# Layer 0's power chains with a scale at every third squaring, and its products entered by two channel chunks at a time

## The chip, the cores and the metric

The kernel runs on one core of a Trainium2 chip. The metric is the device time of one execution in microseconds (us). A core has a matrix engine (TensorE, in the profile PE, its weight loads PEld), a vector engine (VectorE, DVE), an engine for activation functions (ScalarE, ACT), a general engine (GpSimd, POOL) and a queue engine for transfers (SyncE, SP). Each engine takes its instructions in order; they wait for each other by semaphores.

## What is computed

The reference passes x, 8 images of 512 channels by 1024 pixels in float32, through four layers. Only Layer 0 is touched by the change:

```python
z = jnp.einsum('bcn,bcm->bnm', f_x, g_x)          # f_x, g_x: 64 x 1024 for each image
S = jnp.linalg.svd(z, compute_uv=False)
sigma = S[:, 0][:, None, None]                    # the largest singular value
z2 = jnp.einsum('bnm,bcm->bcn', z / sigma, h_x).reshape(b, MID, h, w)
return conv1x1(z2, Wv, bv) + x
```

Layer 1 is a group normalisation and an attention over 1024 pixels, Layer 2 an attention with 128 channels, Layer 3 a convolution of signs.

## The kernel before

**Layer 0's chain.** The largest singular value of z = f'g comes from powers of the 64 x 64 matrix (ff')(gg'), whose largest eigenvalue is sigma squared. Two images stand side by side as blocks of one 128 x 128 matrix (a pair, j), so there are four chains. `chain(j, split)` is a generator. It keeps the current power and its transpose, `cur[:, 0]` and `cur[:, 1]`. A squaring is `products` (two 128x128 matmuls, L1008 and L1009) and `evict` (PSUM to SBUF). In the kernel before, NSTEP is 11: after a first product come 22 squarings, a `yield` after each. Every second one is followed by `diagonal` (VectorE: product with the identity, L1036, and a sum over the row, L1037), and its sum over the partitions, `total`, is a matmul with a 128x1 operand (L1042) and a copy into `tr` (L1043). Its reciprocal (L1069) and the products of it (L1070) scale the next scaled eviction (L1030, or L1026 on ScalarE). At the end the logarithms of the traces (L1080), weighted by `quarters`, give 1/sigma, which scales the weights of the pair's images.

**Who runs the chains.** The chain of the pair whose images come first (`jl`, images 6 and 7) runs in the early stage, in an order of TensorE written out by hand: after each step of the chain some steps of `todo` (weight products L1265, transposes L1117, Gram matrices L1312, biases L1290) are taken as fillers. The other three (`behind = chains()`) run inside the main loop `fast(n)`, one for each image in the order 6, 7, 0, ..., 5: `chore(2)` takes one step of `behind` at every second step of a stage.

**The main loop.** `fast` has the stages scores of Layer 1 (`scores1`, 28 steps of two 128x512 matmuls at L380, here called terms), V (`make_v`, 14 steps at L380), values (`values1`, 14 steps at L547), and then Layers 2 and 3 together with the next image's first products. A term's result is moved out of PSUM by VectorE (`plus`, L337) or by ScalarE. Each bank of PSUM holds 128x512 numbers; the main loop has eight.

**Entering the next image.** `entering(n)` makes Layer 0's last product for image n: `weights0` (L282, evicted at L285 or L287), and then `enter`. For each of four chunks of 128 channels, `enter` does one visit: two matmuls of 64 rows, one for each half of the pixels, on the upper and the lower half of TensorE's rows (L403); then for each half an addition of x (L412) and statistics (L415), and an aggregate (L416). Two further steps make the group normalisation's mean (L423) and its deviation (L430), which give the scale and bias that `normal` applies. In `fast` the six steps are taken at k = 12, 15, 18, 21, 24 and 27 of `scores1`. In the early stage image 6 is entered by `steps`, with fillers between.

Outside the hand-written part and a few marked instructions, a planner sets each engine's order from the program's order and its own estimates. The image's x is loaded on the SP queue after the last image's rest (`rest3`) is done, in four transfers of 512 KB.

Of the kernel before, what the change touches and what calls it, by code (L numbers as in the profile page):

```python
# [8 lines left out]
F32 = mybir.dt.float32  # L9
F16 = mybir.dt.float16  # L10
I32 = mybir.dt.int32
AF = mybir.ActivationFunctionType
# [4 lines left out]
P = 128  # L17
# [47 lines left out]

NSTEP = 11

# [14 lines left out]
def kernel(  # L84
# [36 lines left out]
    def bank():  # L121
        return psum["bank"].tile([P, HF], F32, tag="bank", name="bank")
# [85 lines left out]
    minus_half = const.tile([P, CC], F32, tag="minus_half", name="minus_half")  # L208
    nc.gpsimd.memset(minus_half, -0.5)

    quarters = const.tile([P, NSTEP], F32, tag="quarters", name="quarters")
    for s in range(NSTEP):
        nc.gpsimd.memset(quarters[:, s : s + 1], 0.25**s)

    def vec(name):
        return ct[:, COL[name] : COL[name] + CC]
# [174 lines left out]

    weights = {}

    def enter(xt, f, pv):

        st = stat.tile([P, CC, NH, 6], F32, tag="st1", name="st1")
        mv = stat.tile([P, CC, 2], F32, tag="mv1", name="mv1")
        for oc in range(CC):  # L400
            banks = [bank() for h in range(NH)]
            for h, ps in enumerate(banks):
                mm(  # L403
                    out=ps,
                    lhsT=pv[side(h), bass.ts(oc, P)],
                    rhs=f[side(h), :],
                    start=True,
                    stop=True,
                )
            for h, ps in enumerate(banks):  # L410
                xs = xt[:, oc, half(h)]
                nc.vector.scalar_tensor_tensor(  # L412
                    xs, ps, bvo[:, oc : oc + 1], xs, ALU.add, ALU.add
                )
                nc.vector.bn_stats(st[:, oc, h, :], xs)  # L415
            nc.vector.bn_aggr(mv[:, oc, :], st[:, oc, :, :])  # L416
            yield

        ps = bank()
        mean = stat.tile([P, CC], F32, tag="mean1", name="mean1")  # L420
        dev = stat.tile([P, CC], F32, tag="dev1", name="dev1")
        nc.vector.tensor_tensor(mv[:, :, 0], mv[:, :, 0], bo, ALU.subtract)
        mm(out=ps[:, 0:CC], lhsT=gmat, rhs=mv[:, :, 0], start=True, stop=True)  # L423
# [12 lines left out]
        nc.vector.tensor_tensor(bi, vec("L1_conv_beta"), bi, ALU.subtract)  # L436
        norm[:] = sc, bi
        yield
# [374 lines left out]
    def inverse_sums(env, esum, row):  # L813

        ps = bank()
        for h in range(NH):
            mm(  # L817
                out=ps[side(h), :],
                lhsT=ones2[:, 0:MID],
                rhs=esum[:, half(h)],  # L820
                start=True,
                stop=True,
            )
        r = env["small"].tile([P, HF], F32, tag="rsum", name="rsum", bufs=1)
# [25 lines left out]
    def entering(n):  # L850

        b = order[n]
        f = load_f(b)

        def steps():
            while b // 2 not in ready:
                next(behind)
            if b % 2 == 0:
                for i in (b, b + 1):
                    pvs[i] = weights0(i)  # L860
            yield from enter(resident[b], f, pvs.pop(b))

        return steps()

# [3 lines left out]
    def fast(env, n, hb, ua):  # L868
# [8 lines left out]
        def chore(every):  # L877
            count[0] += 1
            if count[0] % every == 0:
                next(behind, None)  # L880

        es = [None] * NT
        for k, _ in enumerate(scores1(env, hb, ua, es)):
            if rest3 and k % 2 == 0:
                if next(rest3[0], "end") == "end":
                    rest3.pop()
                    if more and order[n + 1] not in resident:
                        resident[order[n + 1]] = load_x(order[n + 1])
            if n == 0 and k == 2:
                weights["o"] = sums_of(quarters_of(wo, chunks, cols2), [so[:, i] for i in range(3)], True)  # L890
            if n == 0 and k == 6:
                tp = quarters_of(sbw["tpg"], chunks, [slice(0, P), slice(P, 2 * P)])
                weights["tp"] = sums_of(tp, [sp[:, i] for i in range(3)], True)
            if k == 8 and more:
                ahead = entering(n + 1)
            if k >= 11 and k % 3 == 0:
                next(ahead, None)
            if not rest3:
                chore(2)
        for _ in ahead:  # L900
# [94 lines left out]
    def chain(j, split):  # L995
# [1 line left out]


        ff, gg, gh = (gm[j][:, i, :] for i in range(3))
        tr = spin.tile([P, NSTEP + 1], F32, tag="tr", name="tr")  # L1000

        def column(name):
            return spin.tile([P, 1], F32, tag=name, name=name)
# [26 lines left out]
                    nc.vector.tensor_scalar(dst, ps, r, again, ALU.mult, ALU.mult)  # L1030
            return cur

        def diagonal(u, v):
            d = spin.tile([P, P], F32, tag="diag", name="diag", bufs=1)
            t = column("tj")
            nc.vector.tensor_tensor(d, u, v, ALU.mult)  # L1036
            nc.vector.tensor_reduce(t, d, AX.X, ALU.add)  # L1037
            return t

        def total(t, s):  # L1040
            ps = bank()
            mm(out=ps[:, 0:1], lhsT=mask2, rhs=t, start=True, stop=True)  # L1042
            nc.vector.tensor_copy(tr[:, s : s + 1], ps[:, 0:1])  # L1043

        t = diagonal(ff, gg)
        got = products(gg, ff)
        total(t, 0)
        r = column("r")
# [10 lines left out]
        t = None  # L1059
# [18 lines left out]
        ln = spin.tile([P, NSTEP], F32, tag="ln", name="ln")  # L1078
        rsig = column("rsig")
        nc.scalar.activation(ln, tr[:, 1:], AF.Ln)  # L1080
        nc.vector.tensor_tensor(ln, ln, quarters, ALU.mult)
        nc.vector.tensor_reduce(rsig, ln, AX.X, ALU.add)
        nc.scalar.activation(rsig, rsig, AF.Exp, scale=-0.125)
        nc.vector.tensor_tensor(rsig, rsig, root, ALU.mult)
        for i in range(2):
            rr = side(i)
# [338 lines left out]
    with tc.manual_schedule(engines={mybir.EngineType.PE}):  # L1425
        steps = entering(0)
        for k, _ in enumerate(chain(jl, True)):
            for _ in range(2 - k % 2 if k <= 2 * NSTEP else 4):
                next(todo, None)
            for args in (next(relus, None),):  # L1430
                if args:
                    relu(*args)
        for k in range(CC + 2):
            next(steps)
            for _ in range(3 if k < CC else 5):
                next(todo, None)
        for _ in todo:
            pass
# [193 lines left out]
```

## Time and profile before

| | |
|---|---|
| median of 14 runs | 1932.19 us (1931.09 to 1933.03) |
| the profiled execution | 1931.56 us |
| its span, first to last instruction | 1929.7 us |
| granted TensorE clock | 0.998 |
| PE busy | 1905.6 us (99%) |
| DVE busy | 1158.4 us (60%) |
| ACT busy | 507.8 us (26%) |
| POOL busy | 229.8 us (12%) |
| DMA | 66.47 MB, 34 GB/s on average |

Busy times are of one profiled execution. A group's line shows the source line, the engine, the operation, output and inputs, the shapes and the count, then busy us and the mean ns of one, then the idle time of the engine just before and what ended it. A float32 matmul stands in the profile as two records, one for each pass. Matmuls are pipelined and their ends are modelled, so durations of neighbours overlap; the distance from start to start is what a piece of work takes. A wait is put down to the semaphore that came last.

### The profile page before, as it was taken

What the parts mean: (1) busy time and instruction counts of PE and PEld (TensorE: products, weight loads), DVE (VectorE), ACT (ScalarE), POOL (GpSimd) and SP (SyncE); (2) the same over time, 40 slices, a digit from 0 to 9 for tenths busy, and PEclk for the clock granted to TensorE, in tenths of its full rate; (3) what the DMA queues carried; (4) which work ended last, traced back from release to release, by engine and by line L of the source; (5) the groups of instructions that cost most, each with busy time, mean ns of one, the idle gap of its engine ahead of it and who ended that gap; (6) DMA issues with size and microseconds to landing.
All of it is one profiled execution on the core that took longest, in us unless ns stands there. A gap on an engine that the chain in (4) does not pass through costs nothing.

```text
span 1929.7 us, 16673 instructions
## 1 busy us (share of the span) xinstructions
PE 1905.6 (99%) x6230; PEld 986.3 (51%) x6230; DVE 1158.4 (60%) x1875; ACT 507.8 (26%) x807; POOL 229.8 (12%) x178
## 2 busy tenths in 40 slices
PE   9999999999999999999999999999999999999997
PEld 3367456544655447454555446544645455544653
DVE  3256677448764687537754676448663775466647
ACT  2141222035222332025212331034202421143114
POOL 0000001200111001300121011201120011201121
PEclk9999999999999999999999999999999999999999
DMA  8420000002000120002000120002000200010001
GB/s 322 152 77 7 1 6 12 1 11 87 17 1 0 33 71 12 1 11 87 17 1 1 33 71 11 1 11 87 11 0 1 86 13 11 0 33 22 11 1 46
DMA packets 27784, 66.47 MB, mean 34 GB/s; under 512 B 4272, under 2 KB 5424, under 8 KB 27056
## 3 DMA queue, kind: packets, MB, share of 16 engines
q1 hardware_dynamic: 26768, 64.90, 10.0%
q8 instruction: 51, 0.84, 0.2%
q10 hardware_dynamic: 864, 0.43, 0.1%
q14 instruction: 37, 0.30, 0.0%
q0 software_dynamic: 64, 0.00, 0.0%
HBM read 38.51 MB, written 18.87 MB: 30 GB/s over the span
## 4 chain that ended last, share of the span: by engine, by line
PE 91%; DVE 7%; ACT 1%; issue 1%; DMA 0%; POOL 0%; DVEq 0%; ACTq 0%
PE bank L380 41%; PE bank L547 20%; PE bank L937 6%; PE bank L796 6%; PE bank L1225 4%; PE bank L648 3%; PE bank L403 2%; PE bank L665 2%; PE bank L1008 1%; PE wide L1265 1%; DVE both L739 1%; DVE both L709 1%; PE bank L1009 1%; PE wide L1312 1%; PE bank L688 1%; PE bank L817 1%
## 5 line engine op out<-in xcount | busy, mean ns | idle before, releaser
L547 PE MATMUL bank<-e,vt 128*128 128x512 f32 x768 | 334.0, 593 | 0.0
L547 PEld LDWEIGHTS bank<-e,vt 128*128 128x128 f32 x768 | 145.0, 190 | 175.4 <-issue 173.2
L380 PE MATMUL bank<-ut,h 128*128 128x512 f32 x384 | 181.3, 596 | 0.0
L337 DVE TENSOR_TENSOR e<-bank,e 128x512 f32<-128x512 f32 x128 | 87.6, 685 | 61.0 <-PE bank L380 60.3
L380 PE MATMUL bank<-us,hs 128*128 128x512 f32 x256 | 122.1, 599 | 1.4 <-DVE us L309 0.5
L380 PEld LDWEIGHTS bank<-ut,h 128*128 128x128 f32 x384 | 71.5, 190 | 85.8 <-issue 83.5
L937 PE MATMUL bank<-e,tpg 128*128 128x512 f32 x256 | 114.7, 595 | 0.0
L796 PE MATMUL bank<-tpg 128*128 128x512 f32 x256 | 114.6, 592 | 0.0
L803 ACT ACTIVATE e<-bank 128x512 f32<-128x512 f32 x128 | 76.4, 597 | 128.5 <-PE bank L796 128.5
L352 POOL TENSOR_TENSOR e<-e 128x512 f32<-128x512 f32 x32 | 44.1, 1379 | 419.5 <-ACT e L331 383.1
L380 PE MATMUL bank<-wo,h 128*128 128x256 f32 x384 | 91.8, 382 | 0.0
L808 DVE TENSOR_TENSOR esum<-esum,e 128x1024 f32<-128x1024 f32 x48 | 58.8, 1226 | 54.5 <-ACT e L803 54.5
L380 PE MATMUL bank<-h,wu 128*128 128x512 f32 x192 | 90.3, 593 | 0.7 <-ACT ut L342 0.7
L337 DVE TENSOR_TENSOR vt<-bank,vt 128x512 f32<-128x512 f32 x64 | 44.1, 688 | 70.4 <-PE bank L380 70.0
L937 PEld LDWEIGHTS bank<-e,tpg 128*128 128x128 f32 x256 | 48.1, 190 | 63.2 <-issue 63.1
L796 PEld LDWEIGHTS bank<-tpg 128*128 128x128 f32 x256 | 48.6, 190 | 60.7 <-issue 60.5
L352 POOL TENSOR_TENSOR ut<-ut 128x512 f32<-128x512 f32 x16 | 21.8, 1360 | 478.2 <-ACT ut L333 478.2
L380 PEld LDWEIGHTS bank<-wo,h 128*128 128x128 f32 x384 | 71.6, 190 | 13.5 <-ACT vt L331 4.1
L380 PEld LDWEIGHTS bank<-us,hs 128*128 128x128 f32 x256 | 46.7, 190 | 56.1 <-issue 46.4
L676 ACT ACTIVATE sg<-xt,rb 128x512 f16<-128x512 f32 x64 | 45.0, 718 | 103.7 <-DVE xt L667 100.2
L825 DVE RECIPROCAL rsum<-bank 128x512 f32<-128x512 f32 x15 | 50.4, 3357 | 28.6 <-PE bank L817 28.6
L380 PE MATMUL bank<-ut,hs 128*128 128x512 f32 x128 | 63.2, 606 | 0.0
(325 smaller groups left out, 3085.2 us busy)
## 6 DMA issues: line engine op xcount, KB each, us to landing
xt<-in_x SPq DMA_DIRECT2D x55, 512.0 KB
out<-both SPq DMA_DIRECT2D x63, 256.0 KB
rfull<-rsum SPq DMA_DIRECT2D x60, 128.0 KB
f_dram<-f SPq DMA_DIRECT2D x8, 256.0 KB
fb<-f_dram SPq DMA_DIRECT2D x8, 256.0 KB
w<-in_w SPq DMA_DIRECT2D x1, 1024.0 KB
q<-in_w_q SPq DMA_DIRECT2D x1, 1024.0 KB
k<-in_w_k SPq DMA_DIRECT2D x1, 1024.0 KB
```

Source lines behind the costliest of these rows:

```text
L337: nc.vector.tensor_tensor(dst, ps, u, ALU.add)
L352: nc.gpsimd.tensor_tensor(c22, c22, c12, ALU.add)
L380: mm(out=ps[:, q * w : (q + 1) * w], lhsT=lt(ka, kb, q, k), rhs=rhs(ka, kb, q, k), start=first and q == 0 and k == 0, stop=last and k == 1 ...
L547: mm(out=ps, lhsT=a[:, t, bass.ts(r_, P)], rhs=e[t], start=first and t == 0, stop=last and t == NTH - 1, skip_group_check=True,)
L648: mm(out=ps[:, i, :], lhsT=xt[:, cc, bass.ts(4 * h + i, P)], rhs=sbw["tpg"][:, cc, 2 * P : 3 * P], start=cc == 0, stop=cc == CC - 1,)
L676: nc.scalar.activation(sg[:, cc, :], xt[:, cc, half(h)], AF.Sign, bias=rb3[:, cc : cc + 1])
L796: mm(out=ps, lhsT=pt[:, 0, bass.ts(t, P)], rhs=tt[:, 0, half(h)], start=True, stop=True,)
L803: nc.scalar.activation(e[:, half(h)], ps, AF.Exp, scale=float(P) ** -0.5)
L808: nc.vector.tensor_tensor(esum, esum, e, ALU.add)
L825: nc.vector.reciprocal(r, ps)
L937: mm(out=banks[h], lhsT=gt[:, t, :], rhs=es[t][:, half(h)], start=t == 0, stop=t == NT - 1,)
L1225: mm(out=banks[i][side(h), :], lhsT=w0[i][:, cc, :], rhs=xt[:, cc, half(h)], start=cc == 0, stop=cc == CC - 1,)
```

## The change

In the chain NSTEP becomes 6. A scaled squaring comes at every third one; there are 20 squarings and 8 totals. The eviction is scaled by the reciprocal of one trace, twice (`r, r`). At the end two sums are taken in one go, the trace of the power and that of the power with its transpose, and one matmul of two columns totals them; the weights of the logarithms (`shares`) combine the two bounds. In the early stage the fillers behind each step follow the new steps. In `entering` there is a `yield` between the weights and the first visit, and for all images but the first entered `enter` makes two visits of two channel chunks (four matmuls, four banks) instead of four of one. In `fast` its steps are taken at k = 10 (the weights), 13 and 20 (the visits) and 27 (the mean) of `scores1` and at k = 5 of `make_v` (the deviation), and no chore is done at k = 13 to 15 and 20 to 22.

```diff
-NSTEP = 11
+NSTEP = 6
...
-    quarters = const.tile([P, NSTEP], F32, tag="quarters", name="quarters")
-    for s in range(NSTEP):
-        nc.gpsimd.memset(quarters[:, s : s + 1], 0.25**s)
+    shares = const.tile([P, NSTEP + 2], F32, tag="shares", name="shares")
+    last = 0.25 * 0.125**NSTEP
+    for s, share in enumerate(
+        [0.125 ** (s + 1) for s in range(NSTEP)] + [-0.5 * last, 0.75 * last]
+    ):
+        nc.gpsimd.memset(shares[:, s : s + 1], share)
...
-    def enter(xt, f, pv):
+    def enter(xt, f, pv, visits=CC):
...
-        for oc in range(CC):
-            banks = [bank() for h in range(NH)]
-            for h, ps in enumerate(banks):
+        n = CC // visits
+        for v in range(visits):
+            banks = [(oc, h, bank()) for oc in range(v * n, (v + 1) * n) for h in range(NH)]
+            for oc, h, ps in banks:
                 mm(
...
-            for h, ps in enumerate(banks):
+            for oc, h, ps in banks:
                 xs = xt[:, oc, half(h)]
...
                 nc.vector.bn_stats(st[:, oc, h, :], xs)
-            nc.vector.bn_aggr(mv[:, oc, :], st[:, oc, :, :])
+                if h:
+                    nc.vector.bn_aggr(mv[:, oc, :], st[:, oc, :, :])
             yield
...
                     pvs[i] = weights0(i)
-            yield from enter(resident[b], f, pvs.pop(b))
+            yield
+            yield from enter(resident[b], f, pvs.pop(b), 2 if n else CC)
...
-            if k >= 11 and k % 3 == 0:
+            if k in (10, 13, 20, 27):
                 next(ahead, None)
-            if not rest3:
+            if not rest3 and k not in (13, 14, 15, 20, 21, 22):
                 chore(2)
-        for _ in ahead:
-            pass
...
                 r = inverse_sums(env, esum, n)
+            if k == 5:
+                next(ahead, None)
             chore(2)
+        for _ in ahead:
+            pass
...
-        for s in range(1, NSTEP + 1):
-            cur = evict(products(cur[:, 0], cur[:, 1]))
+        for s in range(NSTEP + 1):
+            got = products(cur[:, 0], cur[:, 1])
+            if s:
+                total(t, s)
+                r = column("r")
+                nc.vector.reciprocal(r, tr[:, s : s + 1])
+                if split:
+                    r2 = column("r2")
+                    nc.vector.tensor_tensor(r2, r, r, ALU.mult)
+                cur = evict(got, r, r, r2 if split else None)
+            else:
+                cur = evict(got)
             yield
-            got = products(cur[:, 0], cur[:, 1])
-            if t is None:
-                cur = evict(got)
-            else:
-                total(t, s - 1)
-                r, r2, r4 = column("r"), column("r2"), column("r4")
-                nc.vector.reciprocal(r, tr[:, s - 1 : s])
-                nc.vector.tensor_tensor(r2, r, r, ALU.mult)
-                if split:
-                    nc.vector.tensor_tensor(r4, r2, r2, ALU.mult)
-                cur = evict(got, r2, r2, r4)
-            t = diagonal(cur[:, 0], ident)
-            yield
-        total(t, NSTEP)
+            for more in range(2 if s < NSTEP else 1):
+                cur = evict(products(cur[:, 0], cur[:, 1]))
+                if more:
+                    t = column("tj")
+                    diagonal(cur[:, 0], ident, t)
+                yield
+        t = spin.tile([P, 2], F32, tag="td", name="td")
+        diagonal(cur[:, 0], ident, t[:, 0:1])
+        diagonal(cur[:, 0], cur[:, 1], t[:, 1:2])
+        total(t, NSTEP + 1, 2)
...
-            for _ in range(2 - k % 2 if k <= 2 * NSTEP else 4):
+            for _ in range(4 if k == 3 * NSTEP + 3 else 2 if k != 1 and k % 3 < 2 else 1):
                 next(todo, None)
...
-        for k in range(CC + 2):
+        for n in (2, 3, 3, 3, 3, 4, 6):
             next(steps)
-            for _ in range(3 if k < CC else 5):
+            for _ in range(n):
                 next(todo, None)
```

More of the change, by code (lines that the diff above doesn't have):

```diff
@@ L999, in chain @@
         ff, gg, gh = (gm[j][:, i, :] for i in range(3))
-        tr = spin.tile([P, NSTEP + 1], F32, tag="tr", name="tr")
+        tr = spin.tile([P, NSTEP + 3], F32, tag="tr", name="tr")
         def column(name):
@@ L1031, in evict, with diagonal, total @@
             return cur
-        def diagonal(u, v):
+        def diagonal(u, v, t):
             d = spin.tile([P, P], F32, tag="diag", name="diag", bufs=1)
-            t = column("tj")
             nc.vector.tensor_tensor(d, u, v, ALU.mult)
             nc.vector.tensor_reduce(t, d, AX.X, ALU.add)
-            return t
-        def total(t, s):
+        def total(t, s, n=1):
             ps = bank()
-            mm(out=ps[:, 0:1], lhsT=mask2, rhs=t, start=True, stop=True)
-            nc.vector.tensor_copy(tr[:, s : s + 1], ps[:, 0:1])
-        t = diagonal(ff, gg)
+            mm(out=ps[:, 0:n], lhsT=mask2, rhs=t, start=True, stop=True)
+            nc.vector.tensor_copy(tr[:, s : s + n], ps[:, 0:n])
+        t = column("tj")
+        diagonal(ff, gg, t)
         got = products(gg, ff)
@@ L1058, in chain @@
         nc.vector.tensor_tensor(root, root, half_, ALU.mult)
-        t = None
-        for s in range(1, NSTEP + 1):
-            cur = evict(products(cur[:, 0], cur[:, 1]))
-            yield
-            got = products(cur[:, 0], cur[:, 1])
-            if t is None:
-                cur = evict(got)
-            else:
-                total(t, s - 1)
-                r, r2, r4 = column("r"), column("r2"), column("r4")
-                nc.vector.reciprocal(r, tr[:, s - 1 : s])
-                nc.vector.tensor_tensor(r2, r, r, ALU.mult)
-                if split:
-                    nc.vector.tensor_tensor(r4, r2, r2, ALU.mult)
-                cur = evict(got, r2, r2, r4)
-            t = diagonal(cur[:, 0], ident)
-            yield
-        total(t, NSTEP)
-        ln = spin.tile([P, NSTEP], F32, tag="ln", name="ln")
+        for s in range(NSTEP + 1):
[10 more added lines that the diff above has]
+                cur = evict(got)
+            yield
+            for more in range(2 if s < NSTEP else 1):
+                cur = evict(products(cur[:, 0], cur[:, 1]))
+                if more:
+                    t = column("tj")
+                    diagonal(cur[:, 0], ident, t)
[4 more added lines that the diff above has]
+        total(t, NSTEP + 1, 2)
+        ln = spin.tile([P, NSTEP + 2], F32, tag="ln", name="ln")
         rsig = column("rsig")
         nc.scalar.activation(ln, tr[:, 1:], AF.Ln)
-        nc.vector.tensor_tensor(ln, ln, quarters, ALU.mult)
+        nc.vector.tensor_tensor(ln, ln, shares, ALU.mult)
         nc.vector.tensor_reduce(rsig, ln, AX.X, ALU.add)
-        nc.scalar.activation(rsig, rsig, AF.Exp, scale=-0.125)
+        nc.scalar.activation(rsig, rsig, AF.Exp, scale=-0.5)
         nc.vector.tensor_tensor(rsig, rsig, root, ALU.mult)
```

## The prediction

> **What bounds the kernel now.** I read the page's busy shares first, then the waits of TensorE (PE), then its groups by line, and last its timeline around the places that the change touches.
>
> ```profile
> PE 1905.6 (99%) x6230; PEld 986.3 (51%) x6230; DVE 1158.4 (60%) x1875; ACT 507.8 (26%) x807; POOL 229.8 (12%) x178
> ...
> PE   9999999999999999999999999999999999999997
> ...
> PE 91%; DVE 7%; ACT 1%; issue 1%; DMA 0%; POOL 0%; DVEq 0%; ACTq 0%
> ```
>
> TensorE is busy 99% of the span, in every slice, and makes 91% of the chain that ended last. So what the change takes from TensorE's stream shortens the run, and work on the other engines costs nothing until TensorE waits for it. It hardly does: all its waits together are 13 us, and those near the change are
>
> ```profile
> PE bank L423 <- DVE mv L422: 2.2, 5, 0.6
> PE bank L403 <- ACT pv L287: 1.6, 4, 0.7
> ```
>
> The groups concerned (each product shows as two records, one for each pass):
>
> ```profile
> L403 PE MATMUL bank<-fb,pv 64*128 64x512 f32 x128 | 36.9, 641 | 1.6 <-ACT pv L287 1.6
> L1008 PE MATMUL bank<-cur 128*128 128x128 f32 x176 | 36.2, 287 | 0.7 <-ACT cur L1026 0.4 <-DVE cur L1030 0.3
> L1042 PE MATMUL bank<-tj,mask 128*128 128x1 f32 x96 | 13.8, 213 | 0.5 <-DVE tj L1037 0.4
> ```
>
> Durations of overlapping matmuls don't add up to time, so I price by distances between starts in TensorE's timeline (start, duration, line):
>
> ```profile
> 228.67 0.38 PE L1008 MATMUL bank<-cur 128*128 128x128 f32 x2
> 228.89 0.39 PE L1009 MATMUL bank<-cur 128*128 128x128 f32 x2
> 229.12 1.88 PE L380 MATMUL bank<-ut,h 128*128 128x512 f32 x4
> 230.83 1.88 PE L380 MATMUL bank<-us,h 128*128 128x512 f32 x4
> ...
> 240.31 0.38 PE L1008 MATMUL bank<-cur 128*128 128x128 f32 x2
> 240.53 0.39 PE L1009 MATMUL bank<-cur 128*128 128x128 f32 x2
> 240.75 0.28 PE L1042 MATMUL bank<-tj,mask 128*128 128x1 f32 x2
> 240.90 1.96 PE L380 MATMUL bank<-us,hs 128*128 128x512 f32 x4
> 242.70 1.88 PE L380 MATMUL bank<-ut,h 128*128 128x512 f32 x4
> ...
> 244.86 1.88 PE L380 MATMUL bank<-us,h 128*128 128x512 f32 x4
> 246.67 1.13 PE L403 MATMUL bank<-fb,pv 64*128 64x512 f32 x4
> 247.73 1.98 PE L380 MATMUL bank<-ut,hs 128*128 128x512 f32 x4
> 249.55 0.38 PE L1008 MATMUL bank<-cur 128*128 128x128 f32 x2
> ```
>
> A plain term of four records lasts 229.12 to 230.83, 1.715 us, or 0.43 a record. Squaring pair and term last 228.67 to 230.83, 2.16, so a **pair costs 0.445**. With a trace total between them it is 240.31 to 242.70, 2.39, so a **total costs 0.23**. A visit of L403 stretches the term before it to 1.81 (244.86 to 246.67), lasts 1.06, and stretches the next to 1.82: 1.26 in all, while its two products, which run side by side on the two halves of the rows, need 0.86. So a **visit has an overhead of 0.40**. Last, a waiting L423:
>
> ```profile
> 1149.31 1.88 PE L380 MATMUL bank<-us,hs 128*128 128x512 f32 x4
> 1151.60 0.39 PE L423 MATMUL bank<-mv,gmat 128*128 128x4 f32 x2 [0.41 <-DVE mv L422]
> 1151.84 1.96 PE L380 MATMUL bank<-ut,h 128*128 128x512 f32 x4
> ```
>
> It starts 2.29 after the term, where 1.715 would do: the **wait costs 0.57**, more than the 0.41 put down to it.
>
> [...] the 0.40 lies at the entry into the half-row tiles, at their exposed weight load and at the exit. Whether a second pair of half-row products directly behind the first needs no overhead is not in this trace. [...] In the trace the second pass's loads start at 246.78, on the same rows, 0.11 after the first pass's; and the 128x64 column tiles of L1225 stream 32 records in 7.0 us, 0.22 each, with no overhead between pairs. So I take none, and bound it by the full 0.40 (nothing gained).
>
> **The change part by part.**
>
> *Chains.* A chain goes from 22 squarings to 20 and from 12 totals (0 to 11) to 8 (0, six scaled steps, one of two columns at the end). Four chains: 8 pairs x 0.445 = **3.6**; 16 totals x 0.23 = **3.7**. VectorE loses a total's copy, reciprocal and product with each of them, which nobody waits for; a scaled step has one product of 0.24 less before its eviction. At the end of a chain there are two diagonals in one go (0.29 + 0.28 each) with only one filler of 0.93 before the total in the first chain: the wait there, 0.43 now, grows by about **0.5**. The three later chains have eight 128x512 products in that place, 6.9 us, which cover it. POOL's memsets (11 to 8) lie at the start under the loads.
>
> *Visits.* For seven batches two visits of four products take the place of four of two: 14 fewer x 0.40 = **5.6**, between 0 and 5.6. Batch 0 keeps four.
>
> *The yield after the weights.* L282 now stands one step or more ahead of the first visit. Three times L403 waits for its eviction by ScalarE behind a half term: 472.92 - 471.49 - 0.95 = 0.48 each, 1.4; in the first batch L282 and L403 stand 1.79 apart instead of 1.06, 0.73, of which a new mode change takes 0.40. Together **1.7**.
>
> *The statistics.* The last visit is at step 20 and L423 at step 27, seven terms later instead of three. The four waits in the batches without a chain go, 4 x 0.57 = **2.3**; the first batch keeps its own (three fillers behind the last visit as before). L430 moves into the V stage, behind 24 V products; its operand needs only L423's result and a few small VectorE instructions. VectorE's 3.36 us reciprocal and a POOL power of 1.4 us, between two additions of 1.3, come into its way to the scale and bias, and V's sums (L337) are queued behind VectorE's wait for the power; but the first use of the scale stands seven V terms, 12 us, later, and TensorE asks for those sums' banks only some terms on. I take nothing.
>
> *What is late next.* A visit now hands VectorE four evictions and four statistics at once. By starts in the trace these take 0.66, 0.60 and 0.12 (aggregate) each, 5.3 us together, and two sums of 1.2 and a difference of 0.6 stand among them in the built order. Counted from the end of the term before the visit, the reading of vd (L337) ends 10.8 us on; TensorE wants that bank again after the visit (2.1) and six terms, at 12.4. So 1.6 us of slack without a chain. With one, VectorE has another 0.3 to 1.1 us of diagonal or scaling there, and TensorE 0.9 us of pairs; the scaled copy that the next pair needs comes at about 11.5 against 11.4. I allow **0.5** for all of this. PSUM: four banks at once of eight; the next user of the first visit bank comes eight banks later, over 6 us on. The chores left out around a visit move chain steps to later terms and don't change the count; all three chains (66 steps) still end before the batches that need them (2, 4 and 6). DMA: the first visit comes one term later than now but takes two chunks of x; its loads are issued from 1113.57 to 1118.07 and the visit falls at about 1127, the bulk of the bytes lying before 1126. SP's other transfers keep their order.
>
> **Sum.** 3.6 + 3.7 + 5.6 + 1.7 + 2.3 - 0.5 - 0.5 = 15.9 us. The profiled execution took 1931.56 (span 1929.7 and 1.9 around it), so 1915.7; the median of the runs is 0.6 above it, so the forecast is **1916.3**.
>
> **Rivals.**
> 1. *The second half-row pair hides nothing* (its load waits for the first): a merged visit costs 2.52 instead of 2.12 and the 5.6 is gone, or half of it, if only entry and exit are saved. Time 1919 to 1922. [...] Against: the load at 246.78. Chance 0.14.
> 2. *VectorE is late behind each visit*: in-order evictions hold back vd's read by 1 us beyond the slack at some ten of the fourteen visits, loss 10, time 1926. For it: the slack of 1.6 is small. Against: in the densest stretch now (1145.9 to 1151.5) VectorE ran without a gap and TensorE lost only L423's 0.57. Chance 0.08.
> 3. *Slower*: the same place, but decisive once VectorE is over 1.4 us beyond the slack at every visit (14 x 1.4 = 20 us, against 15.9 gained); at 2 us it is 28 lost and 1944. It takes 3.6 us more VectorE work before vd than I count, which no row shows. Chance 0.03.
> 4. *The first chain is held by its own latency*, since only one filler of 0.8 stands behind plain steps: up to 0.5 at each of ten steps, time 1921. Against: now, one filler behind a plain step leaves no wait (124.55). Chance 0.05.
> That the change doesn't do what it says is ruled out by the built order: 84 pairs instead of 92, 32 totals instead of 48, visits of four.
>
> **Numbers.** Main case 0.70. The range of 1912 to 1924 takes in the main case with all small waits gone, rivals 1 and 4, and leaves out rivals 2 and 3. A measurement of this kernel tells 0.2%, 3.9 us, from no change. Faster by more than that: cases 1 and 4, the main one and most of 2, 0.93; within it 0.04; slower 0.03.
>
> **What would show it.** TensorE's busy time falls by 10 to 13 us; L1008 has 160 records of cur and the totals 64. Right: a visit of eight records lasts about 1.92 from its start to the next term's. Wrong: 2.1 or more there. L423's waits drop from five to one and those for pv vanish. Rival 2 or 3 would show as new waits of L380 for VectorE's L337 or L412 in the waits of TensorE. A gain under 8 us would make the account wrong.

## The result and the profile after

The changed kernel takes **1914.70 us** (median of 6 runs, 1914.00 to 1915.37) against 1932.32 (28 runs of the kernel before beside it): a ratio of 0.9909, 95% interval 0.9899 to 0.9919. The forecast was 1916.3. The profiled execution took 1914.53, 17.03 less than the profiled one before; the sum had said 15.9.

Lines have moved. In the changed kernel the terms are L385 (before: L380), the half-row products L409 (L403), the squaring L1020 and L1021, the total L1052, the mean L430 (L423), the reading of vd L342 (L337).

The page of the changed kernel: first busy shares, then TensorE by slices, then the chain that ended last.

```profile
PE 1891.4 (99%) x6166; PEld 979.6 (51%) x6166; DVE 1126.3 (59%) x1761; ACT 510.3 (27%) x811; POOL 224.3 (12%) x175
...
PE   9999999999999999999999999999999999999997
...
PE 92%; DVE 6%; issue 1%; ACT 1%; DMA 0%; POOL 0%; DVEq 0%; ACTq 0%
```

The bound is the same: TensorE, in every slice. Its busy time fell from 1905.6 to 1891.4, 14.2 us, more than the 10 to 13 that the prediction gave as a sign; the other 2.8 us of the gain are waits that went. The waits of TensorE (engine, line, what it waited for; us in total, times, longest):

```profile
PE bank L1052 <- DVE td L1048: 1.1, 1, 1.1
PE quad L1133 <- DVE xt L418: 0.7, 1, 0.7
...
PE bank L430 <- DVE mv L429: 0.6, 1, 0.6
...
PE bank L1020 <- DVE cur L1036: 0.3, 1, 0.3
```

The mean's five waits of 2.2 us are one of 0.6, that of the first image; the four waits for pv are gone; none of L385 is for L342 or for the additions of x. New is a wait of 0.7 of the early stage's transposes (L1133) for an addition of x. The groups by shape:

```profile
L409 PE MATMUL bank<-fb,pv 64*128 64x512 f32 x128 | 32.3, 618 | 0.0
L1020 PE MATMUL bank<-cur 128*128 128x128 f32 x160 | 32.2, 283 | 0.3 <-DVE cur L1036 0.3
L1052 PE MATMUL bank<-tj,mask 128*128 128x1 f32 x56 | 7.9, 211 | 0.0
...
L1052 PE MATMUL bank<-td,mask 128*128 128x2 f32 x8 | 1.2, 222 | 1.1 <-DVE td L1048 1.1
```

160 records of cur instead of 176 and 56 + 8 of the totals instead of 96; L409 has its 128 records still. Last, a merged visit in TensorE's timeline (start, duration):

```profile
245.08 1.88 PE L385 MATMUL bank<-ut,hs 128*128 128x512 f32 x4
246.89 1.99 PE L409 MATMUL bank<-fb,pv 64*128 64x512 f32 x8
248.81 1.99 PE L385 MATMUL bank<-ut,h 128*128 128x512 f32 x4
250.63 1.88 PE L385 MATMUL bank<-us,hs 128*128 128x512 f32 x4
```

From the visit's start to the next term's it is 248.81 - 246.89 = 1.92, with the terms beside it stretched to 1.81 and 1.82, as in a visit of two products. The second two products add 1.92 - 1.06 = 0.86, which is what two products cost with nothing lost.

One caution for all comparisons of single profiled executions: up to its first transpose (L1207), before any chain, TensorE has the same work in all kernels here, but in five traces it comes there at 91.50 (the visits alone), 91.71 (before), 92.14 (the changed kernel), 92.31 (the visits alone, the product with one tensor input) and 92.83 us (the product back); its wait for the first load alone takes 4.1 to 5.0 over all. A figure that is said to be counted from the first transpose leaves this spread out.

### The profile page after: what moved, and what is told of

Its sections match the earlier page's. It is cut to its first block, busy times and chain, and to the rows that moved or that the text cites. A ratio compares the mean times of both kernels' runs of the same rounds, so it can differ in the third digit from the quotient of the medians.

```text
span 1912.7 us, 16430 instructions
## 1 busy us (share of the span) xinstructions
PE 1891.4 (99%) x6166; PEld 979.6 (51%) x6166; DVE 1126.3 (59%) x1761; ACT 510.3 (27%) x811; POOL 224.3 (12%) x175
## 4 chain that ended last, share of the span: by engine, by line
PE 92%; DVE 6%; issue 1%; ACT 1%; DMA 0%; POOL 0%; DVEq 0%; ACTq 0%
PE bank L385 42%; PE bank L554 20%; PE bank L949 6%; PE bank L803 6%; PE bank L1241 5%; PE bank L655 3%; PE bank L409 2%; PE bank L672 2%; PE wide L1281 1%; DVE both L746 1%; DVE both L716 1%; PE wide L1328 1%; PE bank L1020 1%; PE bank L1021 1%; PE bank L695 1%; PE bank L824 1%
## 5 line engine op out<-in xcount | busy, mean ns | idle before, releaser
L385 PE MATMUL bank<-ut,h 128*128 128x512 f32 x384 | 182.3, 597 | 0.0
L342 DVE TENSOR_TENSOR e<-bank,e 128x512 f32<-128x512 f32 x128 | 87.8, 686 | 81.9 <-PE bank L385 80.8
L385 PE MATMUL bank<-us,hs 128*128 128x512 f32 x256 | 121.5, 597 | 1.4 <-DVE us L314 0.5
L385 PEld LDWEIGHTS bank<-ut,h 128*128 128x128 f32 x384 | 71.4, 190 | 95.6 <-issue 84.0
L385 PE MATMUL bank<-wo,h 128*128 128x256 f32 x384 | 91.8, 382 | 0.0
L385 PE MATMUL bank<-h,wu 128*128 128x512 f32 x192 | 90.3, 593 | 0.7 <-ACT ut L347 0.7
L385 PEld LDWEIGHTS bank<-wo,h 128*128 128x128 f32 x384 | 71.6, 190 | 13.5 <-ACT vt L336 4.1
L342 DVE TENSOR_TENSOR vt<-bank,vt 128x512 f32<-128x512 f32 x64 | 44.1, 689 | 56.2 <-PE bank L385 55.9
L385 PEld LDWEIGHTS bank<-us,hs 128*128 128x128 f32 x256 | 47.1, 190 | 55.0 <-issue 48.3
L1241 PE MATMUL bank<-xt,fg 128*64 128x512 f32 x256 | 59.5, 612 | 4.2 <-DMA fg<-in_w_fg 4.2
```

Of the source, the lines that this page charges most:

```text
L342: nc.vector.tensor_tensor(dst, ps, u, ALU.add)
L385: mm(out=ps[:, q * w : (q + 1) * w], lhsT=lt(ka, kb, q, k), rhs=rhs(ka, kb, q, k), start=first and q == 0 and k == 0, stop=last and k == 1 ...
L1241: mm(out=banks[i][side(h), :], lhsT=w0[i][:, cc, :], rhs=xt[:, cc, half(h)], start=cc == 0, stop=cc == CC - 1,)
```

## The experiments

The theories: (a) TensorE's stream is the bound, and each pair (the two matmuls of a squaring), total and visit has the price that the prediction took; (b) VectorE is hidden only by its slack behind a visit (1.6 us estimated between the reading of vd and TensorE's return to that bank); the rivals are that the second half-row products hide nothing, and that VectorE, 59% busy, hides whatever it is given. The kernel before ran beside each of them: its medians were 1931.87 beside the first four that were run (chains, visits, four visits, one visit) and 1931.99 to 1932.31 beside the others.

### The chains alone

The kernel before with the change in the chain, its weights and the fillers behind its steps; `entering`, `enter` and their places in `fast` as before.

> The kernel before with the new chains alone (20 squarings, 8 totals, its fillers in the first chain); visits, their places and the statistics as before. If time is what TensorE's stream loses: 8 pairs x 0.445 + 16 totals x 0.23 = 7.2 us less, some 0.5 back at the end of the first chain, so 1925.0 to 1926 against 1932.3; the waits of L423 (four of 0.4 us) and of the first visit for pv stay. Rival: the chains lay in shadows and the visits made the gain: 1930 or more.

1925.15 us (1924.57 to 1926.09), ratio 0.9965 (0.9952 to 0.9979). The waits of TensorE, lines shifted once more (L428 is the mean, L408 the visit, L1045 the total):

```profile
PE bank L428 <- DVE mv L427: 2.3, 5, 0.7
PE bank L408 <- ACT pv L292: 1.6, 4, 0.7
PE bank L1045 <- DVE td L1041: 1.1, 1, 1.1
...
PE bank L1013 <- DVE cur L1035: 0.7, 1, 0.7
...
PE bank L1013 <- DVE r_e L235: 0.5, 1, 0.5
```

Gain 6.7, where the prediction's terms give 3.6 + 3.7 - 0.5 = 6.8. The waits of the mean and for pv are whole, so they belong to the other half of the change; the wait for td belongs to this one. But the agreement of the sums is in part luck. From the starts of the same instructions in both traces, the three images with a chain give 4.3, where six pairs and twelve totals would give 5.4: the two waits of the squaring (L1013), 1.1 together, stand neither in the kernel before nor in the changed kernel. The early stage, counted from the first transpose, gives 2.6 instead of 1.3; why was not tried.

### The visits alone

The change in `enter`, `entering`, their places and the early stage's fillers behind image 6; the chains with 22 squarings and 12 totals.

> The kernel before with the old chains (22 squarings, 12 totals), and with the two visits of two channel chunks, the yield behind the weights, the new places of the statistics and the steps without chores. If the parts add up: 5.6 (14 mode changes less) + 1.7 (pv) + 2.3 (L423) = 9.6 us less, 1922.7; with e1 the two gains make 17 us. Rival: the longer chains delay VectorE behind the visits of batches 0 to 2, and up to 3 us come back: 1926.

1925.09 us (1924.89 to 1926.06), ratio 0.9966 (0.9952 to 0.9979): gain 6.8, not 9.6. The main wait that it gave back (L1015 is the squaring, L1037 the scaled eviction on VectorE):

```profile
PE bank L1015 <- DVE cur L1037: 3.9, 4, 1.0
```

All four lie some 12 us behind a visit. Timeline of the engines at the first, whose visit starts at 246.75:

```profile
257.17 1.29 POOL L352 TENSOR_TENSOR e<-e 128x512 f32<-128x512 f32 x1 [13.98 <-ACT e L331]
...
257.26 1.22 DVE L1077 TENSOR_TENSOR r<-r 128x1 f32<-128x1 f32 x1
...
258.52 0.54 DVE L1037 TENSOR_SCALAR cur<-bank,r 128x256 f32<-128x256 f32 x1
...
259.12 0.49 PE L1015 MATMUL bank<-cur 128*128 128x128 f32 x2 [0.93 <-DVE cur L1037]
```

The visit's four evictions and four statistics push VectorE's scaling back to the moment at which POOL adds (L352). There the product of the reciprocal with itself (L1077), one number for each row, takes 1.22 instead of a median of 0.16, and ends when POOL's addition ends, at 258.46; the scaled copy follows, and the next pair waits. The changed kernel has no such product in these three chains (`r, r`). So the halves are not independent: 6.7 + 6.8 = 13.5, against 17.6 for the whole (1932.32 - 1914.70). In the three images with a chain the whole gains 9.0, the chains alone 4.3, and the visits alone lose 1.2; the waits of 3.9 here and of 1.1 there make most of the 5.9 that are missing. In the four images without a chain the visits alone gain all their 6.4. In the early stage, counted from the first transpose, the halves gain 2.6 and 1.4, more than the 1.9 of the whole; that is open. Two kernels tried the reading of the product.

### The visits alone, the product with one tensor input

```diff
-                nc.vector.tensor_tensor(r2, r, r, ALU.mult)
+                nc.vector.tensor_scalar(r2, r, r, None, ALU.mult)
```

> The kernel of the visits alone (old chains), with the product r x r that stands between a reciprocal and its scaled copy done by tensor_scalar (one tensor, the factor as the scalar of each row) in place of tensor_tensor with two tensor inputs. In the trace of the visits alone, all four waits for the scaled copy follow a product that took 1.22 us in place of some 0.16 and ended when an addition on POOL ended. If VectorE's instruction with two SBUF inputs is held by POOL's, this one runs on and the waits of the squaring for the scaled copy (3.9 us) go, or all but 0.5 of them: 1921.2 to 1922. If the visit's evictions and statistics alone make the copy late, it is only 0.1 to 0.2 earlier or not at all: 1925. If any instruction of VectorE is held by POOL's, the product takes over 1 us here too: 1925.

1924.97 us (1924.28 to 1925.16), ratio 0.9962 (0.9948 to 0.9975): no gain, 3 us above the time expected of the product's theory. But in the trace its mechanism is there. At the same place the product now runs through while POOL adds:

```profile
258.21 1.29 POOL L352 TENSOR_TENSOR e<-e 128x512 f32<-128x512 f32 x1 [13.98 <-ACT e L331]
258.30 0.21 DVE L1077 TENSOR_SCALAR r<-r 128x1 f32<-128x1 f32 x1
258.55 0.54 DVE L1037 TENSOR_SCALAR cur<-bank,r 128x256 f32<-128x256 f32 x1
```

None of the 40 products takes over 0.22, and no squaring waits for L1037. By the starts of the same instructions TensorE gains 1.0 at each of the four places. The waits of TensorE tell where these 4.0 went:

```profile
PE bank L1232 <- DMA fg<-in_w_fg: 4.7, 1, 4.7
PE bank L1015 <- DVE r_e L228: 2.7, 2, 1.3
```

Two squarings of the V stage, which the planner set differently around their half terms, wait 2.7 in all, behind VectorE's part in the scale of the normalisation; by the starts they cost 1.5 each. The first load is waited for 0.5 longer (4.2 in the visits alone), and the early stage loses 1.0 with it. So this kernel shows which form of the product is long beside POOL's addition (1.22 with two tensor inputs, 0.21 with one) and what that costs TensorE at these places, but not that its removal alone shortens the run.

### The changed kernel with the product back

```diff
-                if split:
-                    r2 = column("r2")
-                    nc.vector.tensor_tensor(r2, r, r, ALU.mult)
-                cur = evict(got, r, r, r2 if split else None)
+                r2 = column("r2")
+                nc.vector.tensor_tensor(r2, r, r, ALU.mult)
+                cur = evict(got, r2, None, r2)
```

> The changed kernel with the product r x r (two tensor inputs) put back between each reciprocal and its scaled copy, as the old chains have it; TensorE's order around the visits stays, and four places in the V stage shift by one or two half terms. If the visits alone gave back 3.9 us because that product is held by POOL's addition behind the visit, the squaring waits here too for the scaled copy, about 1 us at up to four places: 1915.5 to 1918.6, with products of over 1 us in the trace. If it was the scaling at every second squaring that made the copies meet the visits, the product costs VectorE only 0.16 to 0.24 each: 1914.7 to 1915.2, with no such waits.

1918.01 us (1917.14 to 1918.66), ratio 0.9925 (0.9911 to 0.9939): 3.3 above the changed kernel. Its wait of TensorE, and the timeline at the first of the two places:

```profile
PE bank L1020 <- DVE cur L1040: 1.8, 2, 0.9
```

```profile
479.99 1.29 POOL L357 TENSOR_TENSOR e<-e 128x512 f32<-128x512 f32 x1 [15.24 <-ACT e L336]
480.08 1.22 DVE L1077 TENSOR_TENSOR r<-r 128x1 f32<-128x1 f32 x1
```

At two places behind visits the product, one number for each row, meets POOL's addition again, and by the starts the two images concerned lose 1.2 each, 2.4 in all. The profiled execution, the slowest of the five, is 4.1 above that of the changed kernel (1918.66 against 1914.53), and the other 1.7 is not shown to be the product's: TensorE comes 0.7 later to the first transpose, before any chain, and every run of this kernel takes 2.8 to 3.1 us more than its span, where those of all other kernels take 1.7 to 2.0, which is open. So of the 3.3 between the medians about 1 lies outside the span; the medians of the spans differ by 2.2 (1914.9 against 1912.7). Beside POOL's addition the product takes 1.22 with two tensor inputs, here and in the visits alone, and 0.21 with one; the reason for the difference was not shown.

### Four visits, the rest of the change kept

```diff
-            yield from enter(resident[b], f, pvs.pop(b), 2 if n else CC)
+            yield from enter(resident[b], f, pvs.pop(b))
...
-            if k in (10, 13, 20, 27):
+            if k in (10, 13, 15, 18, 20, 27):
```

> The changed kernel with four visits of one chunk (two matmuls) at steps 13, 15, 18 and 20 of the scores instead of two visits of two; the weights' step, the mean at 27, the deviation in the V stage and the steps without chores stay. [...] 14 x 0.40 = 5.6 us more than the changed kernel, 1920.3, and no wait of L423 comes back. Rival: the places of the statistics made the gain and merging none: 1915.

1920.18 us (1919.71 to 1920.64), ratio 0.9939 (0.9925 to 0.9953). Its group of half-row products:

```profile
L409 PE MATMUL bank<-fb,pv 64*128 64x512 f32 x128 | 36.1, 641 | 0.0
```

By the spans it is 1917.8 - 1912.7 = 5.1 us above the changed kernel, by the medians 5.5: 0.36 to 0.39 for each of the 14 visits merged, where 0.40 was predicted; by the starts in the seven images, without the early stage, it is 5.5. The mean's wait stays one of 0.6, so the later place of the mean doesn't need the merged visits.

### One visit of eight products

```diff
-            yield from enter(resident[b], f, pvs.pop(b), 2 if n else CC)
+            yield from enter(resident[b], f, pvs.pop(b), 1 if n else CC)
...
-            if k in (10, 13, 20, 27):
+            if k in (10, 13, 27):
```

> The changed kernel with one visit of all four chunks (eight matmuls in all eight banks) at step 13. TensorE alone would gain another 7 x 0.40 = 2.8 us: 1911.9 (rival: VectorE is never the bound). My theory of VectorE's slack: its queue behind the visit is 5.3 us longer than now, so vd's reading (L337) ends some 16 us after the term before the visit where TensorE wants the bank at 14: a wait of 2 us in each of seven batches, more with a chain, 14 to 18 us lost against 2.8 gained: 1926 to 1930, with a new wait of L385 for L342.

1926.70 us (1923.86 to 1927.26), ratio 0.9971 (0.9961 to 0.9982): 12 us above the changed kernel, where the seven entries into half-row products and exits saved were estimated at 2.8 less (7 x 0.40). The profiled execution, 1923.86, is the fastest of the eight, 9.3 above; what the others lose beyond that no trace shows. Its waits of TensorE:

```profile
PE bank L385 <- DVE e L342: 6.5, 5, 1.5
...
PE bank L1020 <- DVE cur L1042: 2.3, 1, 2.3
PE bank L1052 <- DVE tj L1048: 2.1, 1, 2.1
```

TensorE is even less busy than in the changed kernel (1889.5 us), and the run is longer. Eight evictions and eight statistics in a row are beyond VectorE's slack, at every image: in the four without a chain the reading of vd is late, by 1.5 each time; in the three with one it is once a sum of the chain, once its scaled copy and once the reading of vd.

### One scaled step more for each chain

```diff
-NSTEP = 6
+NSTEP = 7
```

> The changed kernel with NSTEP 7 for 6: each of the four chains has one scaled step more, three squarings and one total. If squarings cost what the prediction took, 12 pairs x 0.445 + 4 totals x 0.23 = 6.3 us more: 1921.0. If the pairs that stand behind half-row products and totals cost the 0.53 to 0.55 that the changed kernel's trace shows there, 12 x 0.55 + 4 x 0.23 = 7.5: 1922.2. If the chains lay beside other work (TensorE waiting anyway), no change: 1914.7.

1926.62 us (1926.08 to 1927.96), ratio 0.9972 (0.9961 to 0.9983): 11.9 above the changed kernel, more than any of the three cases. From start to start, the records of L1020, L1021 and L1052 take 5.95 us more, and each of the four totals stretches the next term by 0.09: 6.3, as the prediction's prices say. Most of the rest are waits that the changed kernel hasn't:

```profile
PE bank L1020 <- DVE cur L1040: 1.3, 1, 1.3
PE wide L1328 <- DVE ft L1139: 0.9, 1, 0.9
PE bank L385 <- DVE hs L325: 0.9, 1, 0.9
PE bank L385 <- DVE h L460: 0.8, 1, 0.8
PE bank L385 <- ACT e L347: 0.7, 1, 0.7
```

Two of them (h, hs) stand at 195.7 and 201.2, where the early stage ends: the longer chain has used up the fillers there (behind the deviation stand 6 records of L1281, in the changed kernel 16). The first and the last stand at 690.9 and 681.6, where one chain ends and the next begins within the scores of one image, which in the changed kernel falls elsewhere. A further 1.5 us lie behind the last computation: from the start of the last addition on POOL to the end of the span it is 9.0 us in this execution and 7.3 to 7.7 in that of every other kernel here. What makes the last outputs land later there is open.

### The statistics twice

In the merged visits `bn_stats` is done twice for each half, with the same result; TensorE's order stays.

```diff
-                nc.vector.bn_stats(st[:, oc, h, :], xs)
+                for _ in range(2 if visits < CC else 1):
+                    nc.vector.bn_stats(st[:, oc, h, :], xs)
```

> The changed kernel with bn_stats done twice for each half in the merged visits (the second overwrites the first with the same numbers): 4 x 0.60 = 2.4 us more work for VectorE in each of 14 visits, TensorE's order as it was. Theory of the slack (VectorE must have read vd, L342, before TensorE comes to that bank again, with 1.6 us to spare): a wait of L385 of about 0.8 at each of the visits without a chain and about 1.3 at those with one, 14 x 1 = some 12 us, range 6 to 17, so 1927, and waits of L385 for L342 or for L418's line in the profile. Rival (VectorE is busy 59% of the span, so 34 us of work more are hidden): 1914.7, no such waits.

1924.09 us (1923.35 to 1924.96), ratio 0.9957 (0.9944 to 0.9971): 9.4 above the changed kernel, between the theory's 6 and 17 and far from the rival's 0. Its waits of TensorE (lines are one further):

```profile
PE bank L385 <- DVE e L342: 3.3, 8, 0.4
PE bank L1053 <- DVE tj L1049: 2.1, 2, 1.0
...
PE bank L1021 <- DVE cur L1043: 0.7, 2, 0.4
```

Eight waits for vd, one for each visit without a chain, each of 0.41. The slack comes from the starts at one of them, with TensorE's timeline:

```profile
1135.79 1.99 PE L409 MATMUL bank<-fb,pv 64*128 64x512 f32 x8
...
1148.69 1.98 PE L385 MATMUL bank<-ut,hs 128*128 128x512 f32 x4 [0.41 <-DVE e L342]
```

The term that wants vd's bank starts 12.90 behind the visit, instead of 12.33 in the changed kernel: 0.57 later, for 2.4 us of work more, so the slack is about 1.8, near the 1.6 computed. (The 0.41 of idle time would make it 2.0; here, as with the mean's wait in the prediction, 0.57 is lost where 0.41 of idle time is put down to the wait.) In the images with a chain it is the chain's sums and copies that come late.

### The mean where it was, three steps behind the last visit

```diff
-            if k in (10, 13, 20, 27):
+            if k in (10, 13, 20, 23):
```

> The changed kernel with the mean's step at k = 23 of scores1 in place of 27, three steps behind the last visit as it was before the change. In the built order its matmul stands 4.5 terms behind the visit, 4.5 x 1.715 + 1.9 = 9.6 us from the visit's start, and VectorE has its four statistics and the aggregate done at about 10.8: a wait of L430 of about 1.2 at each of seven images, 8 us, so 1923. If VectorE is no later than it was before the change, the old 0.57 at each of seven, 4 us: 1918.7. If the place of the mean does not matter, 1914.7.

1927.24 us (1926.24 to 1928.39), ratio 0.9974 (0.9963 to 0.9984): 12.5 above the changed kernel, more than the 8 expected, and the wait is not the mean's own. Timeline of TensorE around the last visit of an image without a chain:

```profile
1136.49 1.99 PE L409 MATMUL bank<-fb,pv 64*128 64x512 f32 x8
...
1147.01 1.13 PE L385 MATMUL bank<-ut,hs 128*128 128x512 f32 x2 [1.47 <-DVE e L342]
1147.97 0.28 PE L430 MATMUL bank<-mv,gmat 128*128 128x4 f32 x2
```

Here a half term that wants vd's bank stands 1147.01 - 1.47 - 1136.49 = 9.05 us behind the visit. VectorE comes through its statistics, vd and the mean's operand 10.5 after it, as estimated (10.8), so the half term waits, and the mean behind it finds its operand there. Each of the seven images loses 1.7 to 1.8. That the mean's own bank moves the turn of vd's bank forward was argued from the order, not tried by itself. What is shown is that behind a merged visit TensorE has to have some 10.5 us of work that needs neither vd's bank nor the mean's operand.

### Two small things more

Image 6 also makes two visits, and three fillers stand behind the first chain's last squaring.

```diff
-            yield from enter(resident[b], f, pvs.pop(b), 2 if n else CC)
+            yield from enter(resident[b], f, pvs.pop(b), 2)
...
-            for _ in range(4 if k == 3 * NSTEP + 3 else 2 if k != 1 and k % 3 < 2 else 1):
+            for _ in range(4 if k == 3 * NSTEP + 3 else 3 if k == 3 * NSTEP + 2 else 2 if k != 1 and k % 3 < 2 else 1):
...
-        for n in (2, 3, 3, 3, 3, 4, 6):
+        for n in (1, 5, 6, 4, 6):
```

> The changed kernel with two small things more: image 6, the first one entered, also makes two visits of two chunks (two entries and exits less, 2 x 0.40 = 0.8 us), and the first chain has three fillers behind its last squaring for two (the wait of its last total for td, 1.05, should go). 0.8 + 1.05 = 1.85 us less: 1912.9. If the fillers only move a wait elsewhere in the early stage (fewer are left behind the visits), 1913.9 to 1914.7.

1912.62 us (1912.42 to 1913.42), ratio 0.9899 (0.9884 to 0.9915). In its waits of TensorE those for td and for the mean's operand are gone, and one is new:

```profile
PE wide L1328 <- DVE gt L1139: 0.8, 1, 0.8
PE quad L1133 <- DVE xt L418: 0.7, 1, 0.7
```

Since the two had not run beside each other, both ran once more on one chip.

> The changed kernel once more, beside the next one on the same chip: 1914.7 as before; the profile's span within 0.5 us of 1912.7.

> The version with two visits for image 6 too and a third filler ahead of the first chain's last total, once more, beside the changed kernel on the same chip. If its 2 us are its own: about 2 us below the changed kernel in the same call (1912.6 against 1914.7). If they were the spread of two calls: no difference.

The changed kernel 1914.92 (1914.72 to 1915.12), this version 1912.81 (1912.45 to 1913.02): 2.1 us less, with no overlap of the runs; by the starts the early stage, where both edits lie, gives 2.2 and the main loop nothing. It is the fastest of all here, by 1% under the kernel before (0.9899, 0.9883 to 0.9916).

## Why the prediction was right

**What bounds.** TensorE's stream did, and prices taken from start to start of its timeline added up: 15.9 forecast and 17.0 measured, with the forecast of 1916.3 above the median by 1.6. By stages, from the starts of the same instruction in both traces, the early stage gave 1.5 (forecast 1.6; counted from the first transpose it is 1.9), the three images with a chain 9.0 (8.3), the four without 6.6 (6.4).

**Squarings and totals.** Right in size: in the main loop the chains alone gain 4.3 of 5.4, and their two waits of 1.1 make up nearly all of the difference; and the starts give 6.3 of 6.3 for the twelve pairs and four totals of NSTEP 7. That the chains alone come to 6.7 of 6.8 in all is in part luck, as shown there. The 0.7 that the three images gave beyond the forecast is mostly the pair's price where the pair stands directly behind half-row products, the mean, the deviation or another layer's product: 0.52 to 0.55 there instead of 0.445 (254.81 to 255.35 behind L403 in the trace of before), at 15 places before, six of them behind L403, and at eight, none behind a visit, in the changed kernel.

**The visits.** Right: 1.92 for a merged one, and 5.1 to 5.5 of 5.6 by the kernel with four visits. Rival 1 (the second products hide nothing) falls: it wanted 2.1 or more. That the second products need no overhead was the author's estimate, from other places in the trace of before. TensorE's weight loads at the visit shown above:

```profile
246.89 0.30 PEld L409 LDWEIGHTS bank<-fb,pv 64*128 64x128 f32 x4 [0.76 <-issue]
...
247.43 0.19 PEld L409 LDWEIGHTS bank<-fb,pv 64*128 64x128 f32 x2 [0.24 <-issue]
...
247.86 0.19 PEld L409 LDWEIGHTS bank<-fb,pv 64*128 64x128 f32 x2 [0.24 <-issue]
```

Those of the first two products start with the visit, after 0.76 without a load, and those of the second two while it runs. The second two use the same rows as the first and add just their 0.86, so no load is exposed between them. What is saved lies at the entry and the exit (a mode change, in the prediction's words), 0.36 to 0.39 for each visit merged; how it arises in TensorE no trace shows.

**pv and the mean.** Right: 1.6 of waits for pv and four of the mean's five are gone, and the kernel of the chains alone still has them all. The early mean shows why the new place is needed: at the old distance the merged visits cost 12.5 us.

**VectorE's lateness.** The allowance of 0.5 was a term too many, and the largest single miss beside the pairs. Timeline of VectorE in the changed kernel, behind the visit that starts at 1128.98, and of TensorE where it comes back to vd's bank:

```profile
1138.77 0.68 DVE L342 TENSOR_TENSOR e<-bank,e 128x512 f32<-128x512 f32 x1
```

```profile
1128.98 1.99 PE L409 MATMUL bank<-fb,pv 64*128 64x512 f32 x8
...
1141.31 1.88 PE L385 MATMUL bank<-ut,hs 128*128 128x512 f32 x4
```

vd is read by 1139.45, 10.5 after the visit's start (forecast 10.8), and the bank is wanted at 12.3 (forecast 12.4): 1.9 of slack, and 1.8 by the doubled statistics. So nothing was lost, where 1.6 had been computed as slack and a loss of 0.5 allowed. Rivals 2 and 3 had the mechanism right, and the kernels with eight products at once and with doubled statistics show it at work; only the work that it takes is not in the changed kernel.

**The end of the first chain.** The sign was right and the size was somewhat small: the wait for td is 1.05 where 0.43 had been, 0.6 for the 0.5 allowed. Timeline of TensorE in the changed kernel:

```profile
156.25 1.04 PE L1133 MATMUL quad<-ident,g 128*128 128x128 f32 x8
158.34 0.38 PE L1052 MATMUL bank<-td,mask 128*128 128x2 f32 x2 [1.05 <-DVE td L1048]
```

One filler stands ahead of the total and VectorE has two diagonals and two sums to do. The 0.7 of the transposes at 168.7 was not foreseen; it stayed when the fillers there were changed, and neither half of the change alone shows it; its cause was not tried. Rival 4 (plain steps with one filler held by latency) shows in nothing but 0.3 at one step.

**What the prediction did not say.** It wrote that nobody waits for the work that VectorE loses with a scaled step, and took the product there at 0.24. It had named the place, a scaled copy that comes at 11.5 where the next pair needs it at 11.4, but behind a merged visit the product takes 1.22 where POOL adds, and TensorE does wait for it. The trace of before had four such products, three of 0.99 and one of 1.25, the first at 259.94 with POOL adding from 259.65; no wait of TensorE followed from them. The sum stood because the changed kernel has no such product in the main loop's chains, which is luck as far as the prediction goes: with the product the change gains 14.3 by the medians (1932.31 - 1918.01) instead of 17.6, some 2.4 of the difference by the product itself.

## What to carry to other kernels

Where one engine is busy 99% of the span, price an edit from the starts in that engine's timeline, from the term before it to the term after, and check that the other engines keep their slack: here two products at a time became four with nearly 2 us to spare, and eight lost 9 to 12 us. Test a slack by adding work to the engine that is said to have it; a busy share of 59% said nothing about it here, where 2.4 us more at each of 14 visits cost 9.4 us. Keep a short VectorE product with two tensor inputs off a path that runs beside POOL's additions: here one of 128x1 took 1.22 us there, and 0.21 with one tensor input.

## What was not expected of the hardware

A VectorE product of 128x1 with two tensor inputs took 1.22 us while POOL's 128x512 addition ran, and 0.21 when its second operand was a scalar of the row. Half-row products that follow each other directly showed no gap: each two add 0.86 us, and a visit of eight products takes 3.63 from its start to the next term's (246.06 to 249.69 in the kernel with one visit), where 1.06 + 3 x 0.86 is 3.64. And two times outside TensorE's work moved without a known cause: from the start of the last addition on POOL to the end of the span it was 9.0 us with NSTEP 7 and 7.3 to 7.7 in the other profiled executions, and the runs of the kernel with the product back take 1 us more outside their span than all others.
